# Moving basis groups, index loads and pinned copies in a four-layer graph network on one core

## The chip, the cores and the metric

The kernel runs on one core of a Trainium2 chip. The metric is the device time of one execution in microseconds (us), the median of three runs. One core has TensorE (PE in the profile), VectorE (DVE), ScalarE (ACT), GpSimd (POOL) and SyncE (SP); each runs its own list of instructions in order and waits on semaphores for the others. DMA transfers are issued from SP, ACT and POOL, and their data arrives later.

## The reference

A residual network of four graph layers over 512 nodes with 512 features and 16896 edges (each of 8192 pairs in both directions, and 512 loops, sorted by destination):

```python
h = relu(layernorm(x)); x = x + L0(h)   # attention over the edges, then a feed-forward of 1024
h = relu(layernorm(x)); x = x + L1(h)   # linear, then twice: sum over edges, two linears, batch norm over nodes
h = relu(layernorm(x)); x = x + L2(h)   # graph convolution, normalised by degree
h = relu(layernorm(x)); x = x + L3(h)   # two relational layers with gates
# each relational layer has two relations, whose weights are mixed from 30 bases of 512 x 512:
w = einsum("rb,bio->rio", att, basis)
msg[e] = sigmoid(x[col] @ gate_w[r]) * x[col] @ w[r],  r = edge_type[e]
out = segment_sum(msg, row) + x @ root + bias
```

In layer 1 the norm is `(h - mean) * rsqrt(var + eps) * gamma + beta`, with mean and variance over the nodes.

## The kernel before

**Edges become matrices.** The edges are read as indices (`dst`, `src`, `edge_type_2`), 128 to a chunk, 132 chunks. They are loaded one chunk to a row, as tiles of 128 and of 4 rows (`idx`, `idx2`), cast to floats (`kn`, L393), transposed by TensorE into columns (L395) and copied as keys (L397, L398). `look_for_strays` (L406 to L415) tests the keys against limits. VectorE and ScalarE make one-hot rows from the keys (`hd` L544, `hs` L550 and L548), and TensorE multiplies them (L557), so that each 512 x 512 count matrix is a sum over chunks. Every later sum over edges is then a matrix product (`gather`, L918, or L320). At the start `first_norm` and `moments` compute the layer norm of the four tiles of x.

**Stages.** In the trace: startup until 21 us; the count phase until 113, in which the q, k and v projections (L479, L492), first scores and basis steps are placed between counts by `plan`, from the string `line`; eight attention blocks, one to a head, until 182 (`sums` L655, `scores` L628, `values` L670; on VectorE a reciprocal L659 and a product L660); the output projection (`attended`) until 206; the feed-forward (`ff`, L861) until 236; its second product and the norm (`y`, L875) until 277; the linear and first gather of layer 1 until 292.8; two convolutions (l = 0 and 1) until 371; layer 2 until 401; layer 3 until the end. In each convolution `aT` is the copy of the gathered rows (L949 to L954), alternating ScalarE and VectorE; then come conv1 and conv2 products, feature block m after feature block m. Each conv2 block gets its bias (Identity, L981), its batch norm's statistics and Relu (L989); `settle` transposes it (L333) two blocks later.

**The bases.** The two relational layers need 60 bases, about 1 MB each. TensorE combines the first 15 of the first layer and the first 22 of the second, VectorE the others. `USES` (L34) writes out by hand the order in which tiles are read: P for a TensorE tile, V for a VectorE tile. The stream `bases` loads them on SP's queue into a pool of four buffers. Taking tile k starts the load of tile k + 3, and that load waits until its buffer's last reader is done.

- A P tile is used by `basis_step` (L227 to L250): four matrix products of 32 output rows (L244, eight records in the trace) into one PSUM bank. There are eight groups of two steps for the first layer and eight groups of three for the second; the third tile of such a group comes as two DMAs. The last step of a group is followed by a ScalarE copy of the bank (`sums`, L249) and a DMA to memory (L250). There is a single such bank, so the next group's first step waits for the copy. The products are kept in program order.
- A V tile is used by `accumulate`: four VectorE operations (L268), drawn one at a time by `advance(more, n)`. So a V tile can stand half used over several stages.

`basis_step` calls are distributed by hand over the stages: in the count phase (`G` in `line`), before each attention block's `sums`, in `attended`, after the transposes of h1, at two places of the feed-forward, in `y`, behind aT of convolution 0, at the ends of both convolutions, and before layer 3 (L1047).

**Order.** `on(...)` (`keep_in_program_order`) pins an instruction; others are placed by a scheduler. So the order of unpinned copies and transposes on an engine can differ from the source. A gather has two branches, for exact small counts and for the general case; instructions do not move across a branch once they are placed.

Of the kernel before, what the change touches and what calls it, by code (L numbers as in the profile page):

```python
# [8 lines left out]
F32 = mybir.dt.float32  # L9
F16 = mybir.dt.float16  # L10
BF16 = mybir.dt.bfloat16
I32 = mybir.dt.int32
F32R = mybir.dt.float32r
AF = mybir.ActivationFunctionType
# [3 lines left out]
P = 128  # L18
N = 512
D = 512  # L20
T = N // P
E = 16896
# [8 lines left out]
RB = 4  # L31
STEPS = 2
BANKS = 8
USES = "P" * 26 + "VPVVVPPPPVVVPPPVVVVPPPPPPVVVVVVVVVVVV"  # L34
FEW = 4095
LESS = 2.0 ** -12
GW = 32
# [37 lines left out]
def gnn_kernel(ctx: ExitStack, tc: tile.TileContext, out: bass.AP, a: dict):  # L75
# [36 lines left out]
    raw = ExitStack()  # L112
    rp = raw.enter_context(tc.tile_pool(name="raw", bufs=1))

    idx = rp.tile([P, 3, P], I32, name="idx")
    idx2 = rp.tile([NCH - P, 3, P], I32, name="idx2")
    for i, name in enumerate(("dst", "src", "edge_type_2")):
        queue = (nc.sync, nc.sync, nc.scalar)[i]
        queue.dma_start(idx[:, i, :], a[name][0:P * P].rearrange("(c p) -> c p", p=P))
        queue.dma_start(idx2[:, i, :], a[name][P * P:E].rearrange("(c p) -> c p", p=P))  # L120
    x = const.tile([P, T, D], F32, name="x")
    for t in range(T):
        (nc.scalar, nc.sync)[t // 2].dma_start(x[:, t, :], a["x"][t * P:(t + 1) * P, :])
# [100 lines left out]
    wide2 = const.tile([P, 32], F32, name="wide2")  # L224
    sums = []

    def basis_step(n=1):  # L227
        for _ in range(n):
            if len(done) == len(loads):
                return  # L230
            l, n, g = loads[len(done)]
            done.append(n)
            assert USES[bases.at] == "P"
            t = bases.take()
            if g == 0:
                sums[:] = [pbas.tile([P, 512], F32, tag="bas", name="bas")]
            if g < STEPS:
                k, at = FULL * NQ, 32 - 2 * NQ * (g + 1)
                lhsT = wide[l][:k, at:at + 32]
            else:  # L240
                k = STEPS * HALF_OF * NQ
                lhsT = wide2[:k, :]
            for j in range(RB):
                tc.keep_in_program_order(nc.tensor.matmul(  # L244
                    sums[0][32 * j:32 * j + 32, :], lhsT=lhsT,
                    rhs=t[:k, j, :], start=(g == 0), stop=(g == STEPS + l - 1)))
            if g == STEPS + l - 1:
                o = spool.tile([P, 512], F32, tag="sums", name="sums")
                nc.scalar.copy(o, sums[0])  # L249
                nc.scalar.dma_start(summed[l][n], o)  # L250

    def wrel_load(l, r, t):
# [69 lines left out]
    def ts(i):  # L322
        return slice(i * P, (i + 1) * P)

    def on(ins):

        return tc.keep_in_program_order(ins)
# [11 lines left out]
    def stat(name, n=1):  # L339
        return small.tile([P, n], F32, name=name, bufs=3)  # L340

    def moments(mv, v, keep=lambda ins: ins):
        st = stat("st", 6)
        keep(nc.vector.bn_stats(st, v))  # L344
        keep(nc.vector.bn_aggr(mv, st))  # L345
# [41 lines left out]
    key = ep.tile([P, 4, NCH], F32, name="key")  # L387
    p = ps()
    pk = p[:, :3 * NCH].rearrange("p (i c) -> p i c", i=3)
    for ix, c0 in ((idx, 0), (idx2, P)):  # L390
        n = ix.shape[0]
        kn = rp.tile([n, 3, P], F32, name=f"kn{c0}")
        on(nc.vector.tensor_copy(kn, ix))  # L393
        for i in range(3):
            on(nc.tensor.transpose(pk[:, i, c0:c0 + n], kn[:, i, :], ident[:n, :n]))  # L395
    moments(mv4[:, 0, :], x[:, 0, :], on)
    on(nc.vector.tensor_copy(key[:, 0:2, :], pk[:, 0:2, :]))  # L397
    on(nc.vector.tensor_scalar(key[:, 2, :], pk[:, 2, :], 0.0, LESS, op0=ALU.is_equal, op1=ALU.max))  # L398

    stray = ep.tile([P, NCH], F32, name="stray")  # L400
    flag = const.tile([1, 1], I32, name="flag")
# [2 lines left out]
    def look_for_strays():  # L404
        over = rp.tile([P, NCH], F32, name="over")
        on(nc.vector.tensor_tensor(stray, key[:, 0, :], lim[:, 0, :], ALU.is_lt))  # L406
        on(nc.vector.tensor_tensor(over, key[:, 0, :], lim[:, 1, :], ALU.is_ge))
        on(nc.vector.tensor_add(stray, stray, over))
        some = rp.tile([P, 1], F32, name="some")
        on(nc.vector.tensor_reduce(some, stray, AX.X, ALU.max))  # L410
        p = ps()
        on(nc.tensor.matmul(p[0:1, 0:1], lhsT=some, rhs=ones, start=True, stop=True))
        on(nc.vector.tensor_copy(iot, it))
        on(nc.vector.tensor_scalar(key[:, 3, :], key[:, 1, :], -1.0, 0.5, op0=ALU.mult, op1=ALU.add))
        on(nc.vector.tensor_copy(flag, p[0:1, 0:1]))  # L415
        first_norm(0)
        moments(mv4[:, 1, :], x[:, 1, :], on)

    strayed = dram.tile([2, P, T * N], F32, name="strayed")

# [32 lines left out]
    look_for_strays()  # L453
    for t in range(2, T):
        moments(mv4[:, t, :], x[:, t, :], on)
        first_norm(t - 1)
    first_norm(T - 1)
    far_off = const.tile([P, P], BF16, name="far_off")
    on(nc.vector.tensor_scalar(far_off, ident, FAR, None, op0=ALU.mult))
    nc.gpsimd.memset(apart, 1.0)  # L460
# [243 lines left out]
    for i, what in enumerate(line):  # L704
        at = max(at, FIRST + (len(order) - 2 - FIRST) * passes // whole)
        at = next((e for e in ends if e - 6 < at <= e), at)
        if waits is not None:
            plan.setdefault(min(waits, at), []).append(lambda: advance(proj))
            waits = None
        plan.setdefault(at, []).append(takes[what][1])  # L710
        passes += takes[what][0]
        if what == "p":
            halves += 1
            if halves % 2 == 0:
                waits = at + 4
        if line[:i + 1].count(what) == 2 and what in "sS":
            for step in range(3):
                plan.setdefault(at + 7 * step + 7, []).append(lambda j="sS".index(what): advance(shifts[j]))
# [25 lines left out]
    for j, block in enumerate(blocks):  # L744
        block.weigh()
        if j + 1 < len(blocks):
            blocks[j + 1].pairs()
        if j + 2 < len(blocks):
            for _ in blocks[j + 2].scores():
                pass  # L750
        if j:
            blocks[j - 1].values()
        if j + 1 < len(blocks):
            basis_step(2 if j < 4 else 1)
            blocks[j + 1].sums()
        if j + 2 < len(blocks):
            for _ in blocks[j + 2].shift():
                pass
# [61 lines left out]
    def exactly(emit):  # L820
# [3 lines left out]
        with branch.Else():  # L824
            emit(f32, 0)

    def settle(l, h2T, m, xn):

        if l == 0:
            p = flip(h2T, m)  # L830
            nc.scalar.copy(xn[0][:, :, ts(m)], p)
            nc.vector.tensor_sub(xn[1][:, :, ts(m)], p, f32(xn[0][:, :, ts(m)]))
        else:
            nc.vector.tensor_add(x[:, :, ts(m)], x[:, :, ts(m)], flip(h2T, m))
# [21 lines left out]
    for half in range(2):  # L856
        ns = slice(half * NH, (half + 1) * NH)
        for i in range(2):
            for m in range(T):
                p = ps()  # L860
                product(p[:, :NH], [(w[i][:, k, ts(m)], h1T[:, k, ns]) for k in range(T)])  # L861
                at = B1 + T * i + m
                nc.scalar.activation(ff[i][:, m, ns], p[:, :NH], AF.Relu, bias=cols[:, at:at + 1])  # L863
                if half == 0 and i == 0 and m == 2:
                    flip(h1, T - 1, h1T)
                if half or i:
                    advance(more)
            if half == 0:
                basis_step(1)
    w = [weights.take(), weights.take()]  # L870
    b2, g2, be2 = (rows.take() for _ in range(3))
    y, hT = big("A"), big("D")
# [65 lines left out]
    for l in range(2):  # L938
# [14 lines left out]
            else:  # L953
                on(nc.scalar.copy(aT[:, m, :], p))  # L954
        if l == 0:
            basis_step(2)
            advance(more, 3)
        else:
            advance(more, 2)
# [16 lines left out]
        for m in range(T):  # L976
            p = ps()
            product(p, [(w[:, k, ts(m)], h1T[:, k, :]) for k in range(T)])
            at = CB2 + T * l + m
            v = h2T[:, m, :]  # L980
            nc.scalar.activation(v, p, AF.Identity, bias=cols[:, at:at + 1])  # L981
            mean, rstd = stats(v)
            at = T * l + m
            sg = stat("sg")
            nc.vector.tensor_mul(sg, rstd, cols[:, GAM + at:GAM + at + 1])
            off = stat("off")
            nc.vector.tensor_mul(off, mean, sg)
            nc.vector.tensor_sub(off, cols[:, BET + at:BET + at + 1], off)
            nc.scalar.activation(v, v, AF.Relu, bias=off, scale=sg)  # L989
            if m > 1:  # L990
                settle(l, h2T, m - 2, xn)
            if m < 2:
                advance(more)
        if l == 0:
            basis_step(1)
            settle(l, h2T, 2, xn)
            basis_step(2)
            settle(l, h2T, 3, xn)
        else:
            basis_step(1)  # L1000
            settle(l, h2T, 2, xn)
            basis_step(1)
            settle(l, h2T, 3, xn)
            basis_step(1)
            gates = gate_rows(1, [apart.bitcast(F32).rearrange("p t n -> p (t n)")[:, N * r:N * r + N] for r in range(2)])
            next(gates)

# [185 lines left out]
```

## Time and profile before

| What | us |
|---|---|
| Three runs | 525.54, 525.03, 522.33 |
| Median | 525.03 |
| The profiled execution | 527.14 |
| Its span in the profile | 525.3 |
| Around the span | 1.8 |
| TensorE busy | 485.9 (93%) |
| VectorE busy | 402.4 (77%) |
| ScalarE busy | 196.6 (37%) |
| GpSimd busy | 37.4 (7%) |

The mean granted clock of TensorE was 0.997. Times in the text are microseconds from the span's start, with line numbers of the kernel before. In a row of a timeline, the first number is the start and the second the time until the last instruction of the row ended; "x16" counts the instructions; a bracket gives the idle time of the engine before the row and what ended it. Rows of one engine can overlap by a little, as TensorE's products are pipelined. A critical chain or a wait is inferred from semaphore events.

### The profile page before, as it was taken

Reading aid. Unit: us, or ns where it says so; the run is one execution under the profiler, and the core shown is the slowest. Engines: PE = TensorE matmul, PEld = TensorE weight load, DVE = VectorE, ACT = ScalarE, POOL = GpSimd, SP = SyncE. Lnnn points to the kernel's source line nnn. Section 1 sums busy time; section 2 is a strip of 40 time slices with the busy share of each in tenths; the row PEclk is TensorE's granted clock in tenths of the full one; section 3 lists DMA queues with packets and bytes.
Section 4 is the critical chain, followed back from the end, with each engine's and each line's share of the span. In section 5 each row is a group of like instructions: output and inputs, shape, how many; then the busy total and the mean of one; then the engine's idle time right before and its main releaser. Section 6 shows DMA issues by size and latency. Waiting matters only on the chain.

```text
span 525.3 us, 5734 instructions
## 1 busy us (share of the span) xinstructions
PE 485.9 (93%) x2014; PEld 248.7 (47%) x2014; DVE 402.4 (77%) x746; ACT 196.6 (37%) x318; POOL 37.4 (7%) x81
## 2 busy tenths in 40 slices
PE   1798999888999899999999899899699999999996
PEld 1333333334555545784444444644454475446642
DVE  6755477969889778999985597688649999999611
ACT  2786768753354212222421215224623610114000
POOL 6000000000000011110040000000010000000000
PEclk9999999998999999999999999999999999999999
DMA  7998777499896749959571794966932994530011
GB/s 229 267 226 220 189 188 171 118 257 230 208 213 165 156 94 262 288 186 238 128 234 67 243 233 121 365 152 169 251 70 80 305 274 167 171 145 2 0 41 41
DMA packets 43033, 94.06 MB, mean 179 GB/s; under 512 B 2124, under 2 KB 2520, under 8 KB 43000
## 3 DMA queue, kind: packets, MB, share of 16 engines
q1 hardware_dynamic: 34544, 67.77, 48.6%
q0 software_dynamic: 5712, 21.07, 13.9%
q10 hardware_dynamic: 2744, 4.79, 2.8%
q8 instruction: 20, 0.33, 0.3%
q14 instruction: 13, 0.11, 0.1%
HBM read 88.38 MB, written 5.24 MB: 178 GB/s over the span
## 4 chain that ended last, share of the span: by engine, by line
PE 66%; DVE 21%; ACT 9%; POOL 2%; issue 2%; ACTq 0%; POOLq 0%
PE pr L320 15%; PE acc L1101 10%; PE pg L320 7%; PE bas L244 4%; DVE wrel L268 4%; PE ps L479 4%; PE ps L655 4%; PE acc L1067 3%; PE ao L557 3%; ACT hs L548 2%; DVE st L344 2%; PE ps L492 2%; PE ao L670 2%; PE acc L918 2%; DVE sc L660 2%; PE psc L628 2%
## 5 line engine op out<-in xcount | busy, mean ns | idle before, releaser
L268 DVE SCALAR_TENSOR_TENSOR wrel<-basis,scal,wrel 128x1024 f32<-128x1024 f32 x60 | 74.2, 1283 | 1.9 <-DMA basis<-in_basis 1.9
L548 ACT ACTIVATE hs<-iot,key 128x512 f16<-128x512 f16 x75 | 49.1, 713 | 9.9 <-PE ao L557 8.2
L544 DVE TENSOR_SCALAR hd<-iot,key 128x32 f16<-128x32 f16 (+1 forms) x132 | 33.7, 294 | 21.6 <-PE ao L557 21.4
L244 PE MATMUL bas<-basis,wide 120*32 120x512 f32 (+1 forms) x320 | 43.3, 600 | 2.9 <-ACT sums L249 2.1
L268 DVE SCALAR_TENSOR_TENSOR w<-basis,scal,w 128x1024 f32<-128x1024 f32 x32 | 39.4, 1283 | 0.0
L557 PE MATMUL ao<-hs,hd 128*32 128x512 f16 x204 | 26.1, 395 | 3.5 <-DVE Bc L566 1.6
L479 PE MATMUL ps<-bigB,w 128*128 128x512 f32 x56 | 27.8, 618 | 1.0 <-ACT bigD L482 0.6
L352 ACT ACTIVATE sd<-mv,eps 128x1 f32<-128x1 f32 x28 | 8.1, 294 | 53.0 <-DVE mv L345 52.0
L644 ACT ACTIVATE sc<-sc 128x2048 f32<-128x2048 f32 (+1 forms) x10 | 15.7, 1566 | 22.4 <-DVE sc L643 22.3
L320 PE MATMUL pr<-bigE,w 128*128 128x512 f32 x48 | 21.4, 595 | 1.7 <-ACT bigE L954 1.7
L1149 DVE TENSOR_TENSOR u<-acc,x 128x512 f32<-128x512 f32 x4 | 2.8, 693 | 23.5 <-PE acc L1101 23.5
L320 PE MATMUL pr<-bigD,w 128*128 128x256 f32 x88 | 20.2, 380 | 0.0
L550 DVE TENSOR_SCALAR hs<-iot,key 128x512 f16<-128x512 f16 x57 | 20.1, 360 | 0.0
L557 PEld LDWEIGHTS <-hd 128*32 128x32 f16 x204 | 6.2, 94 | 27.5 <-issue 19.4
L630 ACT COPY sc<-psc 128x1024 f32<-128x1024 f32 x16 | 16.1, 1008 | 8.1 <-PE psc L628 8.1
L659 DVE RECIPROCAL rec<-ps 128x256 f32<-128x256 f32 x8 | 14.1, 1757 | 6.4 <-PE ps L655 6.4
L643 DVE TENSOR_TENSOR sc<-sc,half 128x2048 f32<-128x2048 f32 (+1 forms) x10 | 18.6, 1865 | 0.2
L660 DVE TENSOR_TENSOR sc<-sc,rec 128x2048 f32<-128x2048 f32 x8 | 18.3, 2292 | 0.3
L628 PE MATMUL psc<-bigC,bigD 64*128 64x256 f32 x128 | 18.2, 402 | 0.0
L320 PEld LDWEIGHTS pr<-bigD,w 128*128 128x128 f32 x88 | 16.6, 190 | 3.0 <-ACT bigE L863 0.8
L320 PE MATMUL pr<-w,bigE 128*128 128x512 f32 x40 | 17.8, 592 | 0.0
L492 PE MATMUL ps<-w,bigB 128*128 128x512 f32 x32 | 15.9, 618 | 2.0 <-DVE bigE L495 2.0
(312 smaller groups left out, 957.4 us busy)
## 6 DMA issues: line engine op xcount, KB each, us to landing
basis<-in_basis SPq DMA_DIRECT2D x32, 960.0 KB, 9.2
basis<-in_basis SPq DMA_DIRECT2D x23, 1024.0 KB, 9.6
basis<-in_basis SPq DMA_DIRECT2D x16, 448.0 KB
summed<-sums ACTq DMA_DIRECT2D x16, 256.0 KB, 7.2
w<-in_W POOLq DMA_DIRECT2D x4, 1024.0 KB, 7.0
row<-in_rows POOLq DMA_DIRECT2D x12, 256.0 KB, 9.6
wrel<-summed POOLq DMA_DIRECT2D x4, 512.0 KB, 7.9
w<-in_conv_W1T POOLq DMA_DIRECT2D x2, 1024.0 KB, 5.7
```

The costliest lines, as they stand in the source:

```text
L244: tc.keep_in_program_order(nc.tensor.matmul(sums[0][32 * j:32 * j + 32, :], lhsT=lhsT, rhs=t[:k, j, :], start=(g == 0), stop=(g == STEPS + ...
L268: on(nc.vector.scalar_tensor_tensor(to[r][:, i:i + 2, :], t[:, i:i + 2, :], scal[:, at:at + 1], to[r][:, i:i + 2, :], op0=ALU.mult, op1=AL ...
L320: nc.tensor.matmul(p, lhsT=lhsT, rhs=rhs, start=(i == 0), stop=(i == len(pairs) - 1))
L479: on(nc.tensor.matmul(p, lhsT=w[:, k, ts(m)], rhs=made["hT"][:, k, :], start=(k == 0), stop=(k == T - 1)))
L492: on(nc.tensor.matmul(p, lhsT=made["hT"][:, k, ts(t)], rhs=w[:, k, :], start=(k == 0), stop=(k == T - 1)))
L544: keep(nc.vector.tensor_scalar(hd[:, :w], iot[:, GW * groups_of[c][0]:GW * groups_of[c][0] + w], key[:, 0, c:c + 1], key[:, 2, c:c + 1], o ...
L548: keep(nc.scalar.activation(hs, iot, AF.Sign, bias=key[:, 3, c:c + 1]))
L557: keep(nc.tensor.matmul(cnt[b][GW * (g % T):GW * (g % T) + GW, :], lhsT=hd[:, at:at + GW], rhs=hs, start=(c == in_bank[g][b][0]), stop=(c ...
L628: on(nc.tensor.matmul(p[:, b, i, :], lhsT=kT[bs, 2 * q + i, ts(self.mt)], rhs=qT[bs, 2 * q + i, self.ns], start=False, stop=(i == 1)))
L655: on(nc.tensor.matmul(self.total, lhsT=ident, rhs=part, start=(j == 0), stop=(j == len(self.parts) - 1)))
L660: on(nc.vector.tensor_mul(self.sc, self.sc, rec[:, None, :].to_broadcast([P, H, NH])))
L1101: nc.tensor.matmul(self.out[t], lhsT=self.uT[r][:, k, ts(t)], rhs=wrel[r][:, k, :], start=False, stop=(r == 1 and k == T - 1))
```

## The change

1. **Indices.** Each index array is read as 66 rows of 256, two chunks to a row, by one DMA instead of two; one cast for each index instead of one for each of two tiles; six transposes into every second column. The moments of x's tiles 0 and 1 come before the key copies and `first_norm(0)`, `first_norm(1)` before `look_for_strays`; tiles 2 and 3 follow it.
2. **Projection copies.** `waits = at + 4` becomes `at + 2`: a projection's second half is advanced two counts sooner.
3. **Attention blocks.** For j = 0, 1, 2 and 5 one basis step stands before `values()`, and one after it in every round; before, two (j < 4) or one stood after it.
4. **Feed-forward.** Its two basis steps are dropped.
5. **aT of convolution 0.** One basis step instead of two, its `sums` copy pinned behind the aT copies.
6. **Ends of the convolutions.** The second half of a conv2 block (`normed`) is put behind the next block's Identity, which is pinned as the Relu is. The basis steps go from 1 + 2 to 1 + 3 (l = 0), and from 1 + 1 + 1 to 1 + 3 + 2 (l = 1).
7. As 40 steps exist in all, the call before layer 3 (L1047) has two left instead of three. `USES` is rewritten to the new order.

```diff
-USES = "P" * 26 + "VPVVVPPPPVVVPPPVVVVPPPPPPVVVVVVVVVVVV"
+USES = "P" * 25 + "VVVVPPPVVVPPPPVVVVPPPPPPPPVVVVVVVVVVVV"
...
-    idx = rp.tile([P, 3, P], I32, name="idx")
-    idx2 = rp.tile([NCH - P, 3, P], I32, name="idx2")
+    idx = rp.tile([NCH // 2, 3, 2 * P], I32, name="idx")
...
-        queue.dma_start(idx[:, i, :], a[name][0:P * P].rearrange("(c p) -> c p", p=P))
-        queue.dma_start(idx2[:, i, :], a[name][P * P:E].rearrange("(c p) -> c p", p=P))
+        queue.dma_start(idx[:, i, :], a[name].rearrange("(c p) -> c p", p=2 * P))
...
-    def basis_step(n=1):
+    def basis_step(n=1, keep=lambda ins: ins):
...
-                nc.scalar.copy(o, sums[0])
+                keep(nc.scalar.copy(o, sums[0]))
...
-    for ix, c0 in ((idx, 0), (idx2, P)):
-        n = ix.shape[0]
-        kn = rp.tile([n, 3, P], F32, name=f"kn{c0}")
-        on(nc.vector.tensor_copy(kn, ix))
-        for i in range(3):
-            on(nc.tensor.transpose(pk[:, i, c0:c0 + n], kn[:, i, :], ident[:n, :n]))
-    moments(mv4[:, 0, :], x[:, 0, :], on)
+    kn = rp.tile([NCH // 2, 3, 2 * P], F32, name="kn")
+    for i in range(3):
+        on(nc.vector.tensor_copy(kn[:, i, :], idx[:, i, :]))
+        for j in range(2):
+            on(nc.tensor.transpose(pk[:, i, j:NCH:2], kn[:, i, ts(j)], ident[:NCH // 2, :NCH // 2]))
+    for t in range(2):
+        moments(mv4[:, t, :], x[:, t, :], on)
...
+    for t in range(2):
+        first_norm(t)
...
-        first_norm(0)
-        moments(mv4[:, 1, :], x[:, 1, :], on)
...
-        first_norm(t - 1)
-    first_norm(T - 1)
+    for t in range(2, T):
+        first_norm(t)
...
-                waits = at + 4
+                waits = at + 2
...
+        if j in (0, 1, 2, 5):
+            basis_step()
         if j:
             blocks[j - 1].values()
         if j + 1 < len(blocks):
-            basis_step(2 if j < 4 else 1)
+            basis_step()
             blocks[j + 1].sums()
...
-            if half == 0:
-                basis_step(1)
...
         if l == 0:
-            basis_step(2)
+            basis_step(1, on)
             advance(more, 3)
...
-            v = h2T[:, m, :]
-            nc.scalar.activation(v, p, AF.Identity, bias=cols[:, at:at + 1])
-            mean, rstd = stats(v)
...
-            nc.scalar.activation(v, v, AF.Relu, bias=off, scale=sg)
+            on(nc.scalar.activation(h2T[:, m, :], p, AF.Identity, bias=cols[:, at:at + 1]))
+            if m:
+                normed(l, h2T, m - 1, moment)
+            moment = stat("mv", 2)
+            moments(moment, h2T[:, m, :])
...
-        if l == 0:
-            basis_step(1)
-            settle(l, h2T, 2, xn)
-            basis_step(2)
-            settle(l, h2T, 3, xn)
-        else:
-            basis_step(1)
-            settle(l, h2T, 2, xn)
-            basis_step(1)
-            settle(l, h2T, 3, xn)
-            basis_step(1)
+        basis_step(1)
+        normed(l, h2T, 3, moment)
+        settle(l, h2T, 2, xn)
+        basis_step(3)
+        settle(l, h2T, 3, xn)
+        if l:
+            basis_step(2)
```

`normed` holds what stood in the loop: the square root of the variance (ScalarE), reciprocal, product with gamma, offset (VectorE), and the Relu on ScalarE, pinned.

More of the change, by code (lines that the diff above doesn't have):

```diff
@@ L825, in exactly, with normed @@
             emit(f32, 0)
+    def normed(l, h2T, m, mv):
+        at = T * l + m
+        sd = stat("sd")
+        nc.scalar.activation(sd, mv[:, 1:2], AF.Sqrt, bias=eps)
+        sg = stat("sg")
+        nc.vector.reciprocal(sg, sd)
+        nc.vector.tensor_mul(sg, sg, cols[:, GAM + at:GAM + at + 1])
+        off = stat("off")
+        nc.vector.tensor_mul(off, mv[:, 0:1], sg)
+        nc.vector.tensor_sub(off, cols[:, BET + at:BET + at + 1], off)
+        on(nc.scalar.activation(h2T[:, m, :], h2T[:, m, :], AF.Relu, bias=off, scale=sg))
     def settle(l, h2T, m, xn):
@@ L979, in gnn_kernel @@
             at = CB2 + T * l + m
-            v = h2T[:, m, :]
-            nc.scalar.activation(v, p, AF.Identity, bias=cols[:, at:at + 1])
-            mean, rstd = stats(v)
[L983 to L989, printed above, removed]
+            on(nc.scalar.activation(h2T[:, m, :], p, AF.Identity, bias=cols[:, at:at + 1]))
[3 more added lines that the diff above has]
+            moments(moment, h2T[:, m, :])
             if m > 1:
```

## The prediction

> **What bounds the kernel now.** I read four views in this order: the engine totals, to see which engine could be the limit; the chain that ended last, to see whether it is; TensorE's timeline around each edit, for its idle gaps and what ended them; the DMA issues, because every moved step starts a load.
>
> ```profile
> PE 485.9 (93%) x2014; PEld 248.7 (47%) x2014; DVE 402.4 (77%) x746; ACT 196.6 (37%) x318; POOL 37.4 (7%) x81
> ...
> PE 66%; DVE 21%; ACT 9%; POOL 2%; issue 2%; ACTq 0%; POOLq 0%
> ...
> L244 PE MATMUL bas<-basis,wide 120*32 120x512 f32 (+1 forms) x320 | 43.3, 600 | 2.9 <-ACT sums L249 2.1
> ...
> basis<-in_basis SPq DMA_DIRECT2D x32, 960.0 KB, 9.2
> ```
>
> TensorE is busy 93% of 525.3 us and is two thirds of the chain, so 39 us of its idle time and 43.3 us of basis steps (L244, 8 records each) are what the edits can reshape. A step costs about 1 us back to back. The last column of L244 names only ScalarE's copy: **no step waits for a tile today**, although a tile takes 9.2 us from issue to landing. The work in front of each step hides that; whether it still does is the main question.
>
> ```profile
> 131.50 1.06 PE L244 MATMUL bas<-basis,wide 120*32 120x512 f32 x8 [0.71 <-ACT sums L249]
> ...
> 292.80 1.93 PE L244 MATMUL bas<-basis,wide 120*32 120x512 f32 x16
> 296.42 7.13 PE L320 MATMUL pr<-bigE,w 128*128 128x512 f32 x16 [1.69 <-ACT bigE L954]
> ...
> 330.10 0.66 PE L333 MATMUL pg<-ident,bigD 128*128 128x128 f32 x4 [1.60 <-ACT bigD L989]
> 330.51 0.47 PE L320 MATMUL acc<-R,bigA 128*128 128x512 f32 x1
> ...
> 370.64 0.66 PE L333 MATMUL pg<-ident,bigD 128*128 128x128 f32 x4 [1.69 <-ACT bigD L989]
> ```
>
> The brackets are the idle time before a row and its releaser. These are the waits the change aims at.
>
> **Part by part**, against the profiled execution.
>
> *Startup.* The index casts wait for the last index landing (4.62), and the larger of them took 2.36 of the two casts' 2.63 us:
>
> ```profile
> 4.75 2.63 DVE L393 CAST kn<-idx 128x384 f32<-128x384 int32 x2 [3.85 <-DMA idx<-in_src]
> ...
> 5.06 2.16 POOL L179 DMA_DIRECT2D row<-in_rows  x4
> ```
>
> A cast of as many columns on few partitions took 0.35 here, and POOL issued four row loads in just that time. [...] After the change one load per index arrives and three casts start singly, from about 2.9 (dst landed at 2.74, edge types at 2.91), before POOL's row loads; only src comes at about 4.6, and can still meet them. By the 0.35 row the keys come 2.36 − 0.35 = 2.0 earlier; if the last cast locks behind POOL, nothing comes. x's norms, pulled ahead of the stray test (L406 to L410, 1.1 us from 9.12), let x's transposes start sooner: the q projection began at 21.17 behind norms that ended at 15.41 and an iota-and-key wait at 18.84. I take **−2.5**, ends 0 and −3.5. It is not covered by weights: Wq was in at 13.72.
>
> *`waits = at + 2`.* Projection copies leave two counts earlier. TensorE waited 2.0 for them at L492 and 0.8 at L479; against that, counts behind them shift. **−0.5**, ends −1.5 and +1.
>
> *Attention blocks.* A group's second step no longer follows its predecessor's last at once, so the 0.7 us wait for the copy (0.71 above; also 0.70 at 117.16 and 0.70 at 107.42) lies under values(). At j = 0 the following sums wait for z anyway; at j = 5 a step moves into a DVE-bound period (rec to rec 9.35). Two gaps × 0.7 = 1.4: **−1.3**, ends 0 and −1.8.
>
> *ff.* Two steps at 213.54 and 221.64 leave a stretch in which TensorE has no gaps: 2 × 0.99, with DVE close behind: **−1.9**, ends −0.7 and −2.0. They are not saved but moved; they reappear below.
>
> *aT of conv 0.* ScalarE's `sums` copy (294.80) stood ahead of the aT copies and so TensorE waited 1.69 after its two steps. Pinned behind them, with one step instead of two, L320 starts near 293.85 in place of 296.42: **−2.6**, ends −1.0 and −2.7. One step of it reappears below.
>
> *End of conv 0 (normed/settle).* Step counts go from 1 + 2 to 1 + 3. The built order puts step, transpose, steps 2 and 3, transpose, and then the first quarter of step 4 **ahead of the gather's branch**, its other three quarters behind the gather. The step itself would fit in the 1.60 gap. Its tile does not: four buffers, one of them held half used by DVE's `accumulate`, so in the built order of SP's queue the load of tile 4 waits for TensorE to release tile 1. The load that stands there today was issued at 326.08, as soon as step 1 ended, beside a 1 MB weight load (324.89 to 330.63), and landed at 335.15: 9.07 us. DVE's row shows the same landing:
>
> ```profile
> 335.18 1.28 DVE L268 SCALAR_TENSOR_TENSOR wrel<-basis,scal,wrel 128x1024 f32<-128x1024 f32 x1 [1.89 <-DMA basis<-in_basis]
> ```
>
> Today the 7.3 us gather lies in that time. Afterwards the gather stands behind the tile: start 335.2 + 0.2 instead of 330.5 = 4.9, and 0.75 after it: **+5.7**. Ends: a tile in a quiet stretch took 5.3 (434.42 to 439.69), which gives 331.4: +1.6; the third of today's loads took 12.1: +8.7. The deferred `normed` I cost at nothing: Identity of the next m is pinned ahead of Relu of this one, both 0.7 to 0.8 us on a ScalarE that is 37% busy, and only the last Relu (329.23) sets the transpose; its chain of small operations is as long as before. The group's copy (0.58) and its DMA issue (0.33) on ScalarE come with step 3, before that Relu is ready.
>
> *End of conv 1.* 1 + 1 + 1 becomes 1 + 3 + 2. Order: transpose, S1, transpose, S2, S3, transpose, S4, first gather quarter of layer 2, quarter of S5, second gather quarter, rest of S5, S6, then gathers 3 and 4 with the L795 transposes. S4 to S6 again need the buffers of S1 to S3. Today's loads at these places were issued at 367.43, 369.02 and 372.35 and landed at 377.01, 382.00 and 386.97: one queue, about 5 us per tile, under gathers and products. S6 can then end near 388; behind it lie 3 + 5 + 8 transposes (2.0), two gathers (1.84 each): L320 starts near 393.7, in place of 387.42: **+6.3**. Ends: tiles at the 5.7 us of the weight load would cost about +1.5; with S6's load behind all else, +8.3.
>
> *L1047.* One step fewer (2.78 to 1.85). But DVE runs without a break from 401.7 to 420.8, through gates and eight L268, and TensorE already waits 0.39 for it at 420.83. **0**, ends −0.9 and 0.
>
> Sum without the clock: −8.8 + 12.0 = **+3.2**.
>
> *Clock.* TensorE's granted clock fell once before:
>
> ```profile
> 117.20:120.18 2.98, 1.52 (x10) 0.59 (x11) 2.98 (x3) 0.00 (x0) 0.00 (x0) 1.00 0.99 210
> 120.18:123.60 3.42, 3.42 (x9) 2.71 (x9) 3.32 (x4) 0.00 (x0) 0.00 (x0) 0.50 0.98 220
> ```
>
> The columns are length, TensorE's busy time and, third from the end, the clock. After a stretch only half busy, 3.4 us ran at half clock, and the twelve L655 matmuls took 4.54 instead of 2.79: 1.75 lost. [...] The 4.9 us stall at conv 0 meets both, those of conv 1 (some 4 and 3 us) at least the row: 2 × 1.7 = +3.4. The old throttled stretch may go with the 0.70 gap before it; half of 1.75 = −0.9. **+2.5**, ends −1.8 and +5.1.
>
> Total **+5.7**. The profiled execution took 527.14 (span 525.3 and 1.8 around it), 2.1 above the median; I add to the median: 525.0 + 5.7 = **530.7**.
>
> **Rivals.**
> - *Tiles in time* (15%). If a buffer is free one step sooner than I read, or loads land in 5 us, both groups lie in the gaps (1.60; 1.69 + 1.70 + 0.87) and cost about 1 together: −8.8 + 1 − 0.9 = −8.7 → **516.3**. For it: no tile wait exists today. Against: SP's waits in the built order, and 9.07 us at this very place.
> - *Late tiles, no clock loss* (28%). +3.2 with the old throttle half gone → **527.3**. For it: the gaps at 370 to 377 cost no clock.
> - *Forecast* (37%): 530.7, own range 528 to 534.
> - *Late tiles, startup still locked* (15%). src's cast meets POOL's row loads and both tile stalls are at their far ends: −6.3 + 17.0 + 3 → **538.7**.
> - *The groups do nothing for blocks and aT* because DVE sets the pace there, and tiles come in time (5%): −4.9 + 1 + 0 → **521**.
>
> The decision between the first and the others falls at a tile latency of about 4.5 us from step 1's end: below it the stall is nothing, above it each microsecond costs one, at two places.
>
> A measurement of this kernel can tell about 1% (5.25 us) from no change. Faster by that (under 519.8): the first rival and a little: 0.16. Within: the second, the last and the forecast's lower part: 0.32. Slower (over 530.3): 0.52. Range 517.5 to 537: it leaves out half of the first rival and most of the fourth.
>
> **What would show it.** Right: in L244's row a releaser DMA basis with 5 to 12 us in all, at the last step before conv 1's gather and at two steps between layer 2's gathers; the 0.7 waits on `sums` gone from the blocks; 1.69 on bigE gone; the first q projection about 2.5 earlier; half clock after the first stall. Wrong: no wait on basis at all (then the first rival), or a cast row still above 2 us.

## The result and the profile after

The changed kernel takes 543.81 us (median of four runs, 541.19 to 545.68), against 525.22 for the kernel before in the same comparison: ratio 1.0363, 95% interval 1.0298 to 1.0428. It is 18.6 us slower; the forecast was 5.7 us slower, and the range ended at 537. The profiled execution took 545.68, with a span of 543.9.

The page of the changed kernel, engine totals, chain and the row of the basis steps (now L242):

```profile
PE 495.8 (91%) x2014; PEld 252.0 (46%) x2014; DVE 400.5 (74%) x747; ACT 196.2 (36%) x318; POOL 37.6 (7%) x81
...
PE 70%; DVE 17%; ACT 5%; DMA 5%; issue 1%; ACTq 0%; DVEq 0%
...
L242 PE MATMUL bas<-basis,wide 120*32 120x512 f32 (+1 forms) x320 | 47.7, 615 | 14.3 <-DMA basis<-in_basis 11.5
```

There are as many matmuls as before, but TensorE is busy for 10 us more: products take longer where the clock is halved (the gather products behind the first stall start 0.43 us apart at 0.50, 0.23 at 1.00), and two basis steps that were cut in two hold TensorE longer than whole ones (0.98 us for a quarter and 0.99 for the other three at full clock, about 1.0 for a whole one). The other 8.7 us of the loss are idle time. DMA has come into the chain with 5%, and the releaser in L242's last column has become the tile load.

To find the places, I matched the same TensorE products in both traces and subtracted their start times; a difference that changes between two rows was won or lost there. Each column is one execution; in particular, the first 30 us differ by up to 2.2 us between executions whose code there is the same.

| Place (time before) | after minus before, us | what lies in between |
|---|---|---|
| first q projection, 21.2 | +1.1 | startup |
| end of the count phase, 113 | +2.7 | +0.7 before 32 (full clock from 27.3, in the kernel before from 24.6), +0.9 at the counts' waits |
| last attention sums, 179 | +1.3 | blocks: -1.5 |
| output projection, 189 | +2.9 | half clock: +1.7 |
| feed-forward's end, 228 | +0.6 | steps gone: -2.4 |
| `y` stage, 244 | +1.9 | a new wait for VectorE: +1.4 |
| last transposes of convolution 0, 330 | -0.7 | aT: -2.6 |
| conv1 of convolution 1, 337.9 | +9.8 | end of convolution 0: +10.5 |
| products of layer 2, 387.4 | +18.4 | end of convolution 1: +8.5 |
| end | +18.6 | L1047 and layer 3: +0.2 |

TensorE's timeline of the changed kernel at the end of convolution 0 (start, length, instructions; in brackets the idle time before and its releaser):

```profile
329.37 0.66 PE L331 MATMUL pg<-ident,bigD 128*128 128x128 f32 x4 [1.58 <-ACT bigD L839]
335.59 1.89 PE L242 MATMUL bas<-basis,wide 120*32 120x512 f32 x2 [5.57 <-DMA basis<-in_basis]
337.41 0.80 PE L318 MATMUL acc<-R,bigA 128*128 128x512 f32 x1
...
346.68 1.06 PE L242 MATMUL bas<-basis,wide 120*32 120x512 f32 x6
```

The first quarter of step 4 (2 of its 8 records) waits 5.57 us for its tile. Then it occupies TensorE for 1.82 us, about as long as a whole step at half clock (1.87, from 387.18 to 389.05). The gather runs from 337.41 to 346.68, 9.27 us in place of 7.36, and the other three quarters take another 0.99 us behind it. Together these make +10.3 of the +10.5. The tile's load was issued at 325.40, behind step 1, and landed at 335.46.

At the end of convolution 1:

```profile
387.18 1.93 PE L242 MATMUL bas<-basis,wide 120*32 120x512 f32 x8 [5.97 <-DMA basis<-in_basis]
...
392.68 1.04 PE L242 MATMUL bas<-basis,wide 112*32 112x512 f32 x2
393.66 0.50 PE L930 MATMUL acc<-R,bigC 128*128 128x512 f32 x1
...
395.70 1.06 PE L242 MATMUL bas<-basis,wide 112*32 112x512 f32 x6
397.46 1.06 PE L242 MATMUL bas<-basis,wide 120*32 120x512 f32 x8 [0.70 <-ACT sums L247]
```

The fourth step waits 5.97 us. The fifth is split: its two records hold TensorE from 392.68 to 393.66, at full clock, and its six take just as long.

The granted clock (third column from the end) of the changed kernel in four stretches; the first number behind the stretch is its length, the second TensorE's busy time:

```profile
177.48:180.89 3.41, 1.55 (x11) 0.61 (x11) 2.84 (x2) 1.87 (x2) 0.00 (x0) 1.00 0.83 172
180.89:184.31 3.42, 3.42 (x9) 2.70 (x8) 0.00 (x0) 0.00 (x0) 0.00 (x0) 0.50 0.91 345
327.67:331.08 3.41, 0.77 (x8) 0.42 (x4) 1.03 (x6) 1.99 (x3) 0.00 (x0) 1.00 1.02 286
331.00:341.00 10.00, 5.41 (x11) 3.00 (x12) 4.00 (x4) 0.00 (x0) 0.00 (x0) 0.50 0.96 289
```

The first tile stall begins at 330.03. The clock halves one microsecond later, at 331.08, and stays so until 341.32; TensorE worked in 5.4 us of these ten. Around the second stall it is the same, from 382.28 to 392.52. The stretch at 181, behind the last wait for z (a sum of weights that VectorE makes for the attention sums), was at full clock before:

```profile
178.20:181.61 3.41, 2.49 (x12) 2.20 (x12) 0.86 (x2) 1.28 (x1) 0.00 (x0) 1.00 0.92 192
181.61:185.03 3.42, 3.42 (x21) 1.90 (x20) 2.98 (x2) 0.00 (x0) 0.00 (x0) 1.00 0.73 176
```

### The profile page after: what moved, and what is told of

The parts are those of the page before. It is cut to its first block, busy times and chain, and to the rows that moved or that the text cites. A ratio compares the mean times of both kernels' runs of the same rounds, so it can differ in the third digit from the quotient of the medians.

```text
span 543.9 us, 5729 instructions
## 1 busy us (share of the span) xinstructions
PE 495.8 (91%) x2014; PEld 252.0 (46%) x2014; DVE 400.5 (74%) x747; ACT 196.2 (36%) x318; POOL 37.6 (7%) x81
## 4 chain that ended last, share of the span: by engine, by line
PE 70%; DVE 17%; ACT 5%; DMA 5%; issue 1%; ACTq 0%; DVEq 0%
PE pr L318 13%; PE acc L1104 10%; PE pg L318 8%; PE bas L242 5%; PE ps L654 5%; DVE wrel L266 4%; PE ps L478 4%; DMA basis<-in_basis 4%; PE acc L930 3%; PE ao L556 3%; PE acc L1070 3%; PE ao L669 2%; PE psc L627 2%; PE ps L491 2%; ACT hs L547 2%; PE acc L318 2%
## 5 line engine op out<-in xcount | busy, mean ns | idle before, releaser
L242 PE MATMUL bas<-basis,wide 120*32 120x512 f32 (+1 forms) x320 | 47.7, 615 | 14.3 <-DMA basis<-in_basis 11.5
L556 PE MATMUL ao<-hs,hd 128*32 128x512 f16 x204 | 27.4, 401 | 5.5 <-DVE Bc L565 2.8
L643 ACT ACTIVATE sc<-sc 128x2048 f32<-128x2048 f32 (+1 forms) x10 | 15.7, 1566 | 30.0 <-DVE sc L642 30.0
L350 ACT ACTIVATE sd<-mv,eps 128x1 f32<-128x1 f32 x20 | 5.8, 293 | 49.5 <-DVE mv L343 48.5
L242 PEld LDWEIGHTS bas<-basis,wide 120*32 120x32 f32 (+1 forms) x320 | 8.8, 109 | 28.8 <-issue 14.6
L642 DVE TENSOR_TENSOR sc<-sc,half 128x2048 f32<-128x2048 f32 (+1 forms) x10 | 18.6, 1864 | 0.2
```

The costliest lines, as they stand in the source:

```text
L242: tc.keep_in_program_order(nc.tensor.matmul(sums[0][32 * j:32 * j + 32, :], lhsT=lhsT, rhs=t[:k, j, :], start=(g == 0), stop=(g == STEPS + ...
L556: keep(nc.tensor.matmul(cnt[b][GW * (g % T):GW * (g % T) + GW, :], lhsT=hd[:, at:at + GW], rhs=hs, start=(c == in_bank[g][b][0]), stop=(c ...
L642: on(nc.vector.tensor_sub(s, s, half[:, 0:1, :].to_broadcast([P, H // pieces, NH])))
```

## The experiments

Ratios are to the kernel before, in the same comparison. The changed kernel stands at 1.0363.

| Kernel | median us | ratio, 95% interval |
|---|---|---|
| s1_startup | 528.73 | 1.0058, 1.0031 to 1.0086 |
| s2_loads | 526.19 | 1.0010, 0.9988 to 1.0033 |
| s3_waits | 525.31 | 1.0004, 0.9984 to 1.0023 |
| s4_blocks | 525.10 | 0.9988, 0.9962 to 1.0014 |
| e1_late | 532.26 | 1.0169, 1.0129 to 1.0210 |
| e3_slot | 533.51 | 1.0197, 1.0150 to 1.0244 |
| e4_whole | 541.45 | 1.0336, 1.0286 to 1.0385 |
| e2_fill | 540.32 | 1.0340, 1.0289 to 1.0392 |
| d1_at | 522.82 | 0.9943, 0.9924 to 0.9961 |
| b1_best | 521.43 | 0.9919, 0.9891 to 0.9947 |
| b2_slot | 524.99 | 0.9989, 0.9973 to 1.0006 |

### Startup: s1_startup and s2_loads

s1_startup is the kernel before with part 1 of the change. s2_loads leaves out its pinned order:

```diff
-    for t in range(2):
-        moments(mv4[:, t, :], x[:, t, :], on)
+    moments(mv4[:, 0, :], x[:, 0, :], on)
     on(nc.vector.tensor_copy(key[:, 0:2, :], pk[:, 0:2, :]))
...
-    for t in range(2):
-        first_norm(t)
```

> Before with the startup part alone (index loads, casts, transposes, and the new pinned order of x's moments and norms). Theory A, the pinned order: VectorE stands at the moments of x's tile 1 until that tile lands (2.5 us in the changed kernel), so the key copies do not come earlier, and tiles 2 and 3 are normed later; the q projection starts at 22.3 in place of 21.2 and the time is 1 to 2 us above before (526.5). Theory B, the loss of the changed kernel's count phase (2.7 us by 110) comes from the projection copies: then this kernel equals before or is up to 2 us faster (523.5).

> Before with the index loads, casts and transposes alone; moments, key copies and norms in the old order. Theory A (the pinned order was the loss): keys come some 2.5 us earlier because no POOL lock remains, x's tile 0 no longer stands behind the key copies' wait, and the q projection starts 0.5 to 2 us earlier: 523.5 to 525. Theory B (nothing before x's landing matters, x's last tile sets the start): the q projection starts within 0.3 of before, 525.2.

VectorE in the changed kernel:

```profile
3.21 1.38 DVE L390 CAST kn<-idx 66x256 f32<-66x256 int32 x3 [2.31 <-DMA idx<-in_dst]
...
7.92 0.69 DVE L342 BATCH_NORM_STATS2 st<-x 128x6 f32<-128x512 f32 x1 [2.52 <-DMA x<-in_x]
...
8.74 0.40 DVE L395 COPY key<-psc 128x264 f32<-128x264 f32 x1
```

and in s2_loads:

```profile
3.20 1.39 DVE L390 CAST kn<-idx 66x256 f32<-66x256 int32 x3 [2.30 <-DMA idx<-in_dst]
...
5.31 0.40 DVE L394 COPY key<-psc 128x264 f32<-128x264 f32 x1
```

The casts are done at 4.6 in both, against 7.4 before, as the prediction wanted. But the pinned statistics of x's tile 1 stand ahead of the key copies, and that tile lands at 7.89. So the keys come at 8.74 instead of 5.31, no earlier than the 8.57 of before, and tiles 2 and 3 of x are normed after the stray test. The q projection starts at 22.4 in s1_startup, 21.2 before and 20.0 in s2_loads: the loads gain 1.2, the order loses 2.4. Single starts scatter, but the groups do not overlap: against this one start of before, the six traces with the new loads and the new order lie at +0.1 to +1.5, the four with the old start at -0.8 to 0, and the three with the new loads alone at -1.2 to -0.5. Theory A holds for the start in both runs, with two reservations. The median of s1_startup is up by some 3.0 us, more than the 1 to 2 expected. And the expectation that no lock with POOL remains is not confirmed: in s2_loads three VectorE operations that begin at 7.88, 8.06 and 8.19 take 1.77, 1.59 and 1.47 us (operations of the same kinds behind them 0.27, 0.20 and 0.66) and all end near 9.65. POOL's memset of `apart` ends about there in the changed kernel (7.71 to 9.53), but there the VectorE operations beside it keep their length (statistics 0.70, the keys' copy 0.40), so what held the three is not shown. The whole time of s2_loads does not show its 1.2 us. Its trace ends 2.8 us ahead; it lacks the stretch at half clock at 120 (1.7 us) and has another at 372, where the gather's products from 372.79 to 378.51 start 0.43 us apart in place of 0.23, some 2.7 us by these starts. The medians do not resolve the rest.

### Projection copies: s3_waits

```diff
-                waits = at + 4
+                waits = at + 2
```

> Before with the projection copies two counts earlier alone. In the changed kernel the two waits of the counts for VectorE's counts copy (Bc) grew from 1.11 to 1.72 and from 0.50 to 1.11, and the waits on bigE shrank from 0.70 and 1.33 to none and 1.13. Theory A: the copies now stand ahead of the counts copies on VectorE: +1.2 - 0.9 = +0.3, 525.5. Theory B: those growths come from the startup's shift, and this kernel gains up to 0.9: 524.3.

```profile
41.66 0.39 PE L557 MATMUL ao<-hs,hd 128*32 128x512 f16 x2 [1.72 <-DVE Bc L566]
...
66.31 0.40 PE L557 MATMUL ao<-hs,hd 128*32 128x512 f16 x3 [1.11 <-DVE Bc L566]
```

Both waits grew by 0.6, just as in the changed kernel, from 1.11 and 0.50. The wait of 0.70 on bigE (here a copy of the v projection) went, a wait of 0.75 on a one-hot row came. From 32 to 107 this kernel loses 0.9 against before. That is theory A with a larger size; the medians do not resolve it (0.9 us is 0.17%).

### Attention blocks: s4_blocks

```diff
+        if j in (0, 1, 2, 5):
+            basis_step()
         if j:
             blocks[j - 1].values()
...
-            basis_step(2 if j < 4 else 1)
+            basis_step()
```

> Before with the attention block steps alone. Theory A: the 0.7 us gaps at 131.5 and 142.1 go, one step's own time moves under DVE-bound periods: -1.5 us, and the clock drop at 120.2 stays, because the gap at 117.2 (j = 0, no values between the steps) stays: 523.7. Theory B: VectorE's period (9.35) sets these blocks anyway, gain under 0.5: 525.

The 0.7 us waits at j = 1 and 2 are gone, and the last sums start 1.5 us earlier against the sums at 119.7. But the stretch behind the last wait for z ran at half clock, as in the changed kernel, and gave 1.7 back. Theory A was right on the blocks and does not show in the total; why the clock took it back is worked out below.

### Where the tiles are late: e1_late and e3_slot

e1_late takes the changed kernel and moves four steps behind what they held up:

```diff
-        basis_step(3)
+        basis_step(2 - l)
         settle(l, h2T, 3, xn)
         if l:
-            basis_step(2)
+            basis_step(1)
...
             exactly(emit)
+            basis_step(1)
             advance(more, 3)
...
-        if t == 3:
-            basis_step(3)
+        basis_step(2 if t == 3 else 1)
```

> The changed kernel with the fourth step at the end of convolution 0 put behind the next gather, and the last three of the end of convolution 1 put between the products of layer 2 (one each). Theory A (tile stalls, and what they do to clock and split steps, are the loss of 10.5 + 8.5): waits on basis tiles fall from 11.5 to under 3, no stretch at half clock there, 543.8 - 16 = 528. Theory B (the groups' TensorE time or the deferred norm is the loss): the steps still cost the same, 540 or more.

```profile
L242 PE MATMUL bas<-basis,wide 120*32 120x512 f32 (+1 forms) x320 | 44.9, 614 | 1.4 <-ACT sums L247 1.4
...
335.50 2.48 DVE L266 SCALAR_TENSOR_TENSOR wrel<-basis,scal,wrel 128x1024 f32<-128x1024 f32 x2 [6.97 <-DMA basis<-in_basis]
```

TensorE no longer waits for a basis tile. The ratio fell from 1.0363 to 1.0169, some 10 us where I expected 16. VectorE now waits 6.97 for its own tile (1.89 in the kernel before), and aT of convolution 1 behind it holds TensorE up for 1.60; each product of layer 2 has a step behind it, and two short stretches at half clock remain, near 369 and 380. Theory B, that the groups' own TensorE time is the loss, can't be the main part: the same 40 steps are there, and half of the loss is gone.

e3_slot leaves all steps where they are and changes one line of the changed kernel:

```diff
             if m < 2:
-                advance(more)
+                advance(more, m + 1)
```

> The changed kernel with one more VectorE basis operation drawn in each second convolution product (one line), so that the V tile is used up before the group begins; steps stay where they are. Theory A (the half-used V tile holds the buffer that step 4 needs, so its load waits for step 1): the load now starts before step 1, the 5.6 us wait at the end of convolution 0 goes with its half clock and its split step, about -9 there; at the end of convolution 1 the fourth step's tile is early too and the wait moves to the fifth and sixth, -3 to -6: 529 to 532. Theory B (the queue is bandwidth bound, a load issued earlier lands no earlier): 541 or more.

```profile
326.33 1.07 PE L242 MATMUL bas<-basis,wide 120*32 120x512 f32 x8 [0.71 <-ACT sums L247]
327.33 0.66 PE L331 MATMUL pg<-ident,bigD 128*128 128x128 f32 x4
...
335.10 7.03 PE L318 MATMUL pr<-bigE,w 128*128 128x512 f32 x16
...
375.34 1.88 PE L242 MATMUL bas<-basis,wide 112*32 112x512 f32 x2 [5.94 <-DMA basis<-in_basis]
```

Once the V tile is used up, its buffer takes the tile of step 4: that load is issued at 318.99, ahead of step 1, and lands at 325.57. The 5.57 us wait is gone, step 4 is whole, and from the last transposes to conv1 it is 7.77 us, the same as in the kernel before, with a step more. At the end of convolution 1 the wait moved to the fifth step's tile, as expected, but it stayed as long: nothing came of the 3 to 6 us expected there, and the time missed the 529 to 532. This settles the first stall: it comes from a load that starts late, because a half used tile holds its buffer. That an earlier load would land no earlier (theory B) is out; it took 6.6 us here and 10.1 in the changed kernel.

### The split step: e4_whole

```diff
-            nc.tensor.transpose(p[:, ts(k)], src[:, s, ts(k)], ident)
+            keep(nc.tensor.transpose(p[:, ts(k)], src[:, s, ts(k)], ident))
...
-            p = flip(h2T, m)
+            p = flip(h2T, m, keep=on if m == 3 else lambda ins: ins)
```

> The changed kernel with the last transposes at the ends of the convolutions pinned behind the fourth step, so that this step is whole ahead of conv 1's gather. The wait for its tile stays (5.5 us). Theory A (the four products of a step run side by side, so a quarter alone costs as much as a step): the quarter's 1.8 and the remainder's 1.0 become one step of 1.0 to 1.9: -0.9 to -1.8 at that place. Theory B (a quarter costs a quarter): no change there, 543.8.

```profile
332.62 1.94 PE L242 MATMUL bas<-basis,wide 120*32 120x512 f32 x8 [7.63 <-DMA basis<-in_basis]
334.49 1.12 PE L331 MATMUL pg<-ident,bigD 128*128 128x128 f32 x4
...
344.31 7.03 PE L318 MATMUL pr<-bigE,w 128*128 128x512 f32 x16
```

(The edit reaches convolution 0 alone.) The whole step takes 1.87 at half clock; in the changed kernel the quarter alone took 1.82 at the same clock. That is theory A. From the step's start to conv1 it is 11.69 us, against 12.08: only 0.4 less, because the transposes, which lay in the wait, now follow it, and because the stretch at half clock did not end at the same point. So the total (1.0336) can't be told from the changed kernel's, and what shows it are the two rows and the pair at 392.68 and 395.70.

### Clock or stall: e2_fill

```diff
+            acc = [bank("acc") for _ in range(T)]
+            for i in range(6):
+                on(nc.tensor.matmul(acc[i % T], lhsT=ident, rhs=h1T[:, i % T, :], start=True, stop=True))
             basis_step(3)
```

> The changed kernel with six needless 128x512 products (0.86 us each) into banks that the gather overwrites, standing in the 6 us wait for the fourth step's tile at the end of convolution 1 alone; they add no work where the wait is full length. Theory A (the idle time drops the clock): the granted clock stays 1.0 around 387, that step takes 1.06 in place of 1.93 and the first gather quarter 1.9 in place of 3.6: about -2.5, 541.3. Theory B (half clock comes from something else, the stall is all): same as the changed kernel or up to 1 us slower.

```profile
375.80 5.32 PE L1012 MATMUL acc<-bigB,ident 128*128 128x512 f32 x12
...
382.12 1.04 PE L242 MATMUL bas<-basis,wide 120*32 120x512 f32 x2 [1.00 <-DMA basis<-in_basis]
...
387.23 1.07 PE L242 MATMUL bas<-basis,wide 112*32 112x512 f32 x8 [1.03 <-DMA basis<-in_basis]
...
391.47 1.06 PE L242 MATMUL bas<-basis,wide 120*32 120x512 f32 x8 [1.14 <-DMA basis<-in_basis]
```

With TensorE kept busy, the clock stayed at 1.00 from 361 to 401, where the changed kernel had 0.50 from 382.28 to 392.52: here it was the idle time that dropped it. But from the first step's transposes to layer 2's products it is 29.4 us, against 30.1. The faster gather quarters only wait for the next tiles, 1.03 and 1.14. So at the end of convolution 1 the tiles' landings set the pace, and the half clock cost under 1 us of its 8.5, not the 2.5 expected. No run loads all of these tiles earlier; what that would bring is not shown.

### The aT edit, and what is worth keeping: d1_at, b1_best, b2_slot

```diff
-            basis_step(2 if j < 4 else 1)
+            basis_step(2 if j < 4 or j == 6 else 1)
...
-            basis_step(2)
+            basis_step(1, on)
             advance(more, 3)
```

> Before with one step behind aT of convolution 0 (its copy pinned behind the aT copies) in place of two; the other step goes ahead of the last attention sums, where TensorE waits 1.86 for z. Theory A (the sums copy was in the way of aT): the 1.69 wait on bigE falls under 0.3 and one step's 0.99 leaves the path, the moved step costs nothing: -2.6, 522.6. Theory B (DVE's half of aT or the next tile sets that time): -1.0 or less, 524.3.

```profile
293.11 7.13 PE L320 MATMUL pr<-bigE,w 128*128 128x512 f32 x16
```

d1_at is 0.57% faster (0.39 to 0.76): 3.0 us by the ratio, and 2.8 between 292 and 331 in the trace. No wait on bigE is left. The moved step fits into the last wait for z.

> Before with the index loads and casts (norms in the old order), the attention block steps apart, and the aT edit with its step ahead of the last attention sums; ends of the convolutions, feed-forward and projection copies as before. If the parts add as their traces did: -1.2 - 1.5 - 2.6 = -5.3, 520. If a lost stretch of half clock comes for each gap that moves (as in the runs of the single parts): -2 to -3, 522.5.

b1_best joins d1_at's edits with s2_loads and the blocks apart. It is the fastest of all, 521.43 us, 0.81% under before (0.53 to 1.09), and beats both kernels.

```profile
PE 483.9 (94%) x2014; PEld 248.0 (48%) x2014; DVE 400.7 (77%) x747; ACT 195.8 (38%) x318; POOL 37.5 (7%) x81
...
L242 PE MATMUL bas<-basis,wide 120*32 120x512 f32 (+1 forms) x320 | 43.7, 601 | 2.1 <-ACT sums L247 2.1
```

No basis step waits for a tile. In the trace the product starts are 8.1 us earlier than before in the end; the medians differ by 4.4, for this execution was the fastest of its nine (519.25 us).

> As b1_best, and one of the two feed-forward steps moved to the end of convolution 0, made 1 + 3 there, with the V tile used up by one more VectorE operation and the last transposes pinned behind the steps. Theory A (with its tile there, the fourth step fits into the 1.6 us wait for the Relu): no wait on a basis tile, one more microsecond gone: 519. Theory B (the feed-forward is VectorE bound, so its step was free): equal to b1_best.

Neither theory: b2_slot gave 3.6 us of b1_best's gain back.

```profile
329.40 3.68 DVE L266 SCALAR_TENSOR_TENSOR wrel<-basis,scal,wrel 128x1024 f32<-128x1024 f32 x3 [4.51 <-DMA basis<-in_basis]
333.00 1.28 DVE L951 COPY bigE<-acc 128x512 f32<-128x512 f32 x2
```

The half used V tile was also a cushion. With it used up, the three operations that stand ahead of the aT copies need the next tile, which lands late; VectorE waits 4.51, the aT copies wait behind it, and TensorE waits 2.04 for them. The fourth step, too, waits 0.48 for its tile.

## Why the prediction was right or wrong

**Direction and main mechanism right, size wrong by a factor of three; the terms that failed most are the startup and the end of convolution 0.** Named beforehand and found: the wait on basis tiles at the ends of both convolutions, 11.5 us in two waits (5 to 12 forecast, in three); the -2.6 of aT; the blocks' -1.5 (-1.3); L1047 at nothing (+0.2); half clock at the first stall. The end of convolution 1 was priced at +6.3 and a clock loss of 1.7, 8.0; it cost 8.5. Some of that agreement is luck, for e2_fill leaves under 1 us to the clock. The landings there came 10.9, 15.8 and 20.5 us after the first step began, in the kernel before 10.7, 15.7 and 20.7.

Of the missing 12.9 us, some 12 lie in five terms of the sum:

- **Startup, -2.5, measured +1.1 at the q projection and +1.8 at 32.** The cast's part was right in size: three casts done at 4.6, against 7.4. That the long cast of before was held up by POOL (the prediction's lock) no run shows by itself: it ran from 4.75 to 7.11 beside POOL's row loads (5.06 to 7.22), and the changed kernel's casts, of 66x256 against 128x384 and done before its row loads begin at 5.57, took 0.90, 0.31 and 0.32. I priced the norms "pulled ahead of the stray test" as instructions, and did not ask what the moved instruction waits for: x's tile 1, which landed at 7.89. s1_startup and s2_loads separate the two. Of the +1.8, 0.7 is the later start of the full clock, which differs between executions.
- **Projection copies, -0.5, measured +0.9.** My own upper end was +1. The copies now stand ahead of the counts' copies on VectorE (s3_waits).
- **End of convolution 0, +5.7 and 1.7 for the clock, measured +10.5.** Three sizes were short by about 1 us each. The wait was 5.57 against the 4.7 in the sum, since the load took 10.1 us and not 9.07. I counted a quarter of a split step as a quarter (0.2, and 0.75 for the rest), and it costs as much as a step: 0.98 and 0.99 at full clock. The half clock cost 0.8 more on the quarter (1.82) and 1.9 on the gather, against 1.7.
- **Feed-forward, -1.9, measured -2.4 and +1.4 back.** I wrote "DVE close behind" and took the far end all the same. TensorE arrives earlier at the transposes behind `y`'s first products and waits 1.21 for VectorE. The near end, -0.7, was the better guess.

```profile
245.34 0.63 PE L591 MATMUL pg<-ident,u 128*128 128x128 f32 x4 [1.21 <-DVE u L586]
```

- **Clock, -0.9 for the old stretch, measured 0 and +1.7.** The stretch at 120 stayed: at j = 0 no values() stand between the two steps, so their gap was not touched. A new one came behind the last wait for z.

The rival "late tiles, startup still locked" came nearest in number (538.7). Its two stalls, 17.0 and 3 for the clock, are near the 19.0 measured, but its startup had another cause: the three casts took 1.38 us together, and the order lost what they gained.

"Tiles in time" is dead as written. Its argument, that no tile wait existed, was a statement about the old places of the steps. But its condition was the right one: with the buffer free one step sooner (e3_slot) the first stall is gone.

The sum's +3.4 counts 1.7 for half clock at each end, and takes the lengths of the waits (4.9, some 4 and 3 us) for what decides. No run shows that a wait must reach a length: the clock fell 1.05 and 1.08 us into the two tile stalls, and a wait of 1.85 us sufficed at 181. What the runs showed in its place is 10.24 us at 0.50 at each end, which cost 2.7 at the first (0.8 and 1.9, above) and under 1 at the second. The row of the stretch at 120 pointed the right way, and the 13 traces together tell more. In each of them all changes of the clock lie whole multiples of 3.41 us apart, as on a grid (in the changed kernel the falls at 122.87, 180.89, 331.08 and 382.28 are 17, 44 and 15 such lengths apart). I cut the time into these slots, 1883 at full clock up to the last whole one. In 33 of them TensorE was busy for less than 49%, and the next slot ran at half clock each time; none of the 1831 above 51.5% was followed by half clock, and 2 of the 19 in between were. In the kernel before, the slot ahead of 120.18 was 46% busy, and two of 50% (from 294.26 and 372.76) were followed by full clock; ahead of the changed kernel's four falls TensorE was busy for 45%, 46%, 23% and 48%. A slot at half clock was followed by full clock where TensorE was busy for 92% of it or more (25 slots), and by another at half clock at 84% or less (11).

So what counts in these traces is how a wait lies in the grid. The last wait for z, 1.85 or 1.86 us in all, leaves TensorE 46% busy if it falls into one slot, as from 177.48 to 180.89 above, and 57% or more if an edge parts it. In the four traces without the blocks' edit and with that wait unfilled it began 1.96 to 2.74 us behind an edge and was parted; in the six with the edit, whose blocks are 1.5 us shorter, it began 0.6 to 1.5 us behind one and was not. That is the 1.7 us that the edit of the blocks gave back: half of a slot. Why the starts lie so close together in each group is not shown.

## What to carry to other kernels

Before a step is moved into an idle gap, ask which buffer its data needs, who holds that buffer, and when its load can start: the gap of 1.6 us was no use for a tile that arrived 10 us after the step before it (a wait of 5.57 us). For each moved instruction, list what it waits for and who stands behind it on its engine; the pinned statistics handed their wait for x on to the keys (8.74 in place of 5.31). And look in the built order for a step cut in two by a branch or another stage (each part took as long as a whole one, 0.98 and 0.99 us). Where a gain of 1 to 2 us is at stake, compare traces stretch by stretch: a stretch at half clock hid it in s4_blocks (1.5 us won, 1.7 given back).

## What was not expected of the hardware

- The four products of a basis step, which write 32 rows each, take as long together as one: in the changed kernel one alone holds TensorE for 0.98 us (from 392.68), the other three together for 0.99 (from 346.68), all four for about 1.0 (from 376.21).
- In all 13 traces the clock changed on a grid of 3.41 us, and it halved behind slots in which TensorE was busy for less than about half, with no single wait longer than 1.86 us in some of them. A slot at half clock that is full of work loses 1.7 us, half of its length. The edge, between 49% and 51.5%, is read from these traces alone.
- In the first 24.6 us of the kernel before the records run at half pace (transposes take 0.42 us in place of 0.27, q products 1.06 in place of 0.59), while the clock column says 1.00: the trace's first clock record comes only when full pace begins, at 24.6 there and at 17.1 in s2_loads; that is 1.7 of the 2.9 us by which the latter is ahead at 32.
